# High and low parts of queries and keys side by side in one staging tile, sent to both rows of a pair by one transfer

## The chip, the cores and the metric

The kernel runs on one core of a Trainium2 chip. The metric is the device time of one execution in microseconds (us). The profile names the engines PE (TensorE; PEld is its weight load), DVE (VectorE), ACT (ScalarE), POOL (GpSimd) and SP (SyncE, which here only issues transfers); "SPq" is SyncE's issue queue.

## What is computed

Two layers of a transformer block over x (4 sequences of 512 tokens, width 320) with a context (4 sequences of 1601 tokens, width 192); 20 heads of width 16. Each layer is self-attention, cross-attention and a gated feed-forward, each behind a layer norm and added to x:

```python
h1 = _ln(x, n1_g, n1_b)
x = _attn(h1, h1, q1, k1, v1, o1_w, o1_b, heads) + x
h2 = _ln(x, n2_g, n2_b)
x = _attn(h2, context, q2, k2, v2, o2_w, o2_b, heads) + x
h3 = _ln(x, n3_g, n3_b)
a, g = jnp.split(h3 @ ff_w1 + ff_b1, 2, axis=-1)
return a * jax.nn.gelu(g, approximate=False) @ ff_w2 + ff_b2 + x
```

where `_attn` is `softmax(q @ k.T * 16**-0.5) @ v` per head, then the output projection. All in float32.

## The kernel before, in words

**Units.** The work is a list of units: one for each layer, kind (self or cross), sequence and group of four heads, so 40 self units and 40 cross units, and 8 feed-forward units. `main` runs a unit as a loop over chunks of 128 keys: 4 in a self unit, 13 in a cross unit. Each chunk is two rounds, and a feed-forward unit has 24, which makes 2 x (20 x 8 + 20 x 26 + 4 x 24) = 1552 rounds in the program. A round is also the clock of the schedule: `clock["round"]` counts them, and due times and gaps are given in rounds.

**High and low parts.** Scores need float32 accuracy, but the matmuls of scores run in the single-pass type float32r. So queries and keys are split in two parts, high = the rounded value and low = the rest, and the sum of four products (high and low of the one by high and low of the other) is accumulated. A head has 16 dimensions and owns 32 partitions: each dimension owns a pair of rows. In the key tile `kT` the even row of a pair holds the high part and the odd row the low part. The query tile `q` has two slots `e`: in slot 0 even rows hold high and odd rows low, in slot 1 the other way round. A matmul over 32 rows with slot 0 gives high x high + low x low, and one with slot 1 adds the two mixed products.

**From projection to rows.** Projections come out of PSUM with one row for each dimension, not a pair. ScalarE (`L919` in self units, `L952` in cross units) or, for the keys of a cross unit, VectorE or ScalarE (`L1011`, `L1014`) writes the value into a staging tile, and `split` on GpSimd makes high (`L820`) and low (`L821`) of it. High and low are two tiles of their own, `high` and `low`, two buffers each (`two`), for self units and for the queries of cross units; for the keys of cross units they are two parts, `room["high"]` and `room["low"]`, of one larger tile that the trace calls `stages`. The staging tile of a unit has 64 rows for each thing that is moved: rows 0 to 63 are queries and 64 to 127 keys in a self unit; in a cross unit the two halves of rows are the two halves of the tokens. Transfers then spread the 64 rows over the 128 rows of pairs. Each transfer takes either high or low to every second row:

- self unit: keys 2 transfers (`kT<-high`, `kT<-low`, 128 KB each), queries 4 (two slots, high and low, 128 KB each);
- cross unit: keys 4 (two halves of 801 keys, high and low, 200.2 KB each), queries 8 (two halves of the tokens, two slots, high and low, 64 KB each).

All these are issued at one line, `L869`, in `move`.

**The schedule around it.** `move` doesn't issue at once: it puts a function on one of two lists of the unit (`u.moves["k"]`, `u.moves["q"]`). `carry`, called once a round, issues from these lists in order when the buffer is free (`may`) and a gap has passed (`GAP` = 3 rounds after the split for the first move of a list). It has a room of 4 and each move takes 2, so at most two moves go out in a round; what room is left goes to errands, such as the loads of finished heads and the `nrows` transfers. During start-up (`start["on"]`) moves go out at once, in turn on the queues of SyncE and ScalarE. `u.open` counts a unit's moves that are still to go: 3 in a self unit and 6 in a cross unit, since one move holds two transfers. When it is 0, `u.when` is set to the round, and four rounds later (`at_hand`) `giver` may hand out the unit's first products, the row maxima (`sps` by `L1073` and `L1098`, reduced by VectorE in `L1084`), which run beside the scores (`st` by `L1321`) of the unit before. `staging_free` lets the next projection but one start when a unit's query moves have gone out. The negated row maxima get to the score products as a third matmul with `nrows`, which comes by four small transfers at `L1168` for each unit.

**Order.** The program order on each engine is fixed when the kernel is built, from `pace`, `pick` and the costs written in the code; the chip only waits on semaphores. SyncE's queue takes its transfers strictly in program order: moves, `nrows` (`L1168`), `oway` (`L1188`, finished heads to DRAM), `aT` and `rT` (`L1221`, `L1222`, back from there), context tiles (`L725`, `L758`, `L772`) and weights.

Of the kernel before, what the change touches and what calls it, by code (L numbers as in the profile page):

```python
# [9 lines left out]
F32 = mybir.dt.float32  # L10
# [7 lines left out]
B, N, D = 4, 512, 320  # L18
S2, CTX = 1601, 192
H, DH = 20, 16  # L20
# [3 lines left out]
P = 128  # L24
NQ = N // P
G, HG = 5, 4
GD = HG * DH
SLOT = 32
# [14 lines left out]
HALF = TOK // 2  # L43
# [6 lines left out]
GAP = 3  # L50
# [28 lines left out]
def kernel(ctx: ExitStack, tc: tile.TileContext, x, context, ws, out):  # L79
# [18 lines left out]
    nc = tc.nc  # L98
# [42 lines left out]
    def take_rooms(l):  # L141

        room["layer"] = l

        for i in range(1, 3):
            kbuf[i] = shared.tile([P, KW], F32R, tag=f"kT{i}", name=f"kT{i}")
        qbuf[3] = shared.tile([P, 2, N], F32R, tag="rests", name="q3")
        free = shared.tile([P, NHC * D], F32, tag="second", name="stages")
        at = 0

        def part(n):
            nonlocal at
            at += n
            return free[:, at - n : at]

        room["low"], room["high"] = part(HALF), part(HALF)
        room["in"] = [part(2 * CTX).rearrange("p (c d) -> p c d", d=CTX) for _ in range(2)]
        room["turned"] = [part(2 * CTX).rearrange("p (k w) -> p k w", k=KB) for _ in range(2)]
        room["context"] = [
            w1_flat[:96, 2 * D : 2 * D + 2 * TOK].rearrange("p (k w) -> p k w", k=2),  # L160
            one.tile([96, 2, TOK], F32, tag="ctxT", name="ctxT"),
        ]
# [138 lines left out]
    class Unit:  # L301


        def __init__(self, l, kind, b, g):
            self.l, self.kind, self.b, self.g = l, kind, b, g
            self.cross = kind == "cross"
            self.rows_of = None
            self.nkeys = S2 if self.cross else N
            self.nch = (self.nkeys + P - 1) // P

            self.moves = {"k": deque(), "q": deque()}
            self.moving = {"k": 0, "q": 0}
            self.open = 6 if self.cross else 3
            self.keyed = None
            self.when = None
            self.vmade = [0, 0]

            self.made = {"q": 0, "k": 0, "kv": 0}
            self.scored = 0
            self.valued = 0  # L320
            self.steps = 2 * self.nch if kind != "ff" else 2 * NHC + NQ
            self.before = None
            self.others = []
            self.early = False
            self.own = {}
            self.pairs = self.hT = self.kvT = None
# [5 lines left out]
        @property  # L332
        def q(self):
            if not self.cross and self.m % 4 == 3:
                return kbuf[2][:, N : 3 * N].rearrange("p (e n) -> p e n", e=2)
            return qbuf[3 if self.early else self.m % 3 if self.cross else self.m % 4]

        def places(self):

# [483 lines left out]
    def add_proj(u):  # L823
# [28 lines left out]
            else:  # L852
                add(chain, 0.0, hold, due - 4, yes, lambda: "h" in u.own)

        def staged():
            users.append(u)
            return (two.tile([P, N], F32, tag=n, name=n) for n in ("low", "high"))

        def move(of, pairs, may, gap=0):

# [22 lines left out]
        def keys_free():  # L883
            return not pending["k"]

        def move_queries(high, low, cols, may, gap):
            for e in range(2):
                move(
                    "q", lambda e=e: [(u.q[(e + h) % 2 :: 2, e, cols], t) for h, t in enumerate((high, low))],
                    may, 0 if e else gap,  # L890
                )

        def both(part):

            w = N // 2
            at = part * w
            ps = bank("qkps")
            written(1.4, ps)
            busy("act", 0.4, ps)
            for k, _, n in HK:  # L900
                for f, m in tiles_of(P):
                    column = u.g * GD + f % GD
                    nc.tensor.matmul(  # L903
                        ps[f : f + m, :w],
                        lhsT=wqk[:n, k, f // GD, column : column + m],
                        rhs=first.hT[:n, k, at : at + w],
                        start=(k == 0),
                        stop=(k == 2),
                    )
            if part == 0:  # L910
                u.stage = tuple(staged())
            low, high = u.stage
            if u.i == 0:
                nc.scalar.activation(high[:, at : at + w].bitcast(F32R), ps[:, :w], AF.Copy, scale=scales[:, 0:1])
                nc.vector.scalar_tensor_tensor(
                    low[:, at : at + w], ps[:, :w], scales[:, 0:1], high[:, at : at + w], ALU.mult, ALU.subtract
                )
            else:
                nc.scalar.activation(low[:, at : at + w], ps[:, :w], AF.Copy, scale=scales[:, 0:1])  # L919
            if part == 0:  # L920
                return
            if u.i:
                split(low, high)
            def may():
                return unread() and free()

            move(
                "q", lambda: [(u.kT[h::2, u.k0 : u.k0 + N], t[GD:]) for h, t in enumerate((high, low))], may, GAP,
            )
            move_queries(high[:GD], low[:GD], slice(0, N), may, 0)  # L930
            u.keyed = True
            first.made["q"] += 1
            first.made["k"] += 1

        def queries():

            w = N // 2
            ps = bank("qps")
            written(1.41, ps)
            busy("act", 0.33, ps)  # L940
            for k, _, n in HK:
                for i in range(2):
                    for f in range(GT):
                        nc.tensor.matmul(  # L944
                            ps[(i * GT + f) * SLOT : (i * GT + f + 1) * SLOT, :w],
                            lhsT=wq2[:n, k, u.g * GD + f * SLOT : u.g * GD + (f + 1) * SLOT],
                            rhs=first.hT[:n, k, i * w : (i + 1) * w],
                            start=(k == 0),
                            stop=(k == 2),
                        )  # L950
            low, high = staged()
            nc.scalar.mul(low[:, :w], ps[:, :w], DH**-0.5)  # L952
            split(low[:, :w], high[:, :w])
            for i in range(2):
                rows = slice(i * GD, (i + 1) * GD)
                move_queries(high[rows, :w], low[rows, :w], slice(i * w, (i + 1) * w), unread, 0 if i else GAP)
            u.keyed = True
            first.made["q"] += 1

        def keys_of_context(part):  # L960

            at, w = KCUT[part]
            ps = bank("kps")
            written(0.1 + w * 4 * 2 / 2400, ps)
            for k in range(2):
                for i in range(2):
                    for f in range(GT):
                        nc.tensor.matmul(  # L968
                            ps[(i * GT + f) * SLOT : (i * GT + f + 1) * SLOT, :w],
                            lhsT=wk2[:, k, u.g * GD + f * SLOT : u.g * GD + (f + 1) * SLOT],  # L970
                            rhs=first.kvT[:, k, i * HALF + at : i * HALF + at + w],
                            start=(k == 0),
                            stop=(k == 1),
                        )
            low, high = room["low"], room["high"]
            taken(low[:, at : at + w], ps[:, :w], ps, 0.12 + w * 0.001)
            if part + 1 < len(KCUT):
                return
            split(low, high)

            def half(i):
                to = u.kT[:, i * HALF : (i + 1) * HALF]
                return [(to[h::2], t[i * GD : (i + 1) * GD]) for h, t in enumerate((high, low))]

            move("k", lambda: half(0), free, GAP + 1)
            move("k", lambda: half(1), free)
            first.made["kv"] += 1
# [69 lines left out]
    def max_pairs(u):  # L1057
# [9 lines left out]
        def one_tile(j, t, s):  # L1067
# [4 lines left out]
            def product(e):  # L1072
                nc.tensor.matmul(  # L1073
                    own[0][:, :w],
                    lhsT=u.q[j * SLOT : (j + 1) * SLOT, e, t * P : (t + 1) * P],
                    rhs=u.kT[j * SLOT : (j + 1) * SLOT, u.k0 + at : u.k0 + at + w],
                    start=(e == 0),
                    stop=(e == 1),
# [10 lines left out]
        def rest_tiles(heads):  # L1089
# [5 lines left out]
            def product(t):  # L1095
                for e in range(2):
                    for j, ps in zip(heads, pss):
                        nc.tensor.matmul(  # L1098
                            ps[:, t * w : (t + 1) * w],
                            lhsT=u.q[j * SLOT : (j + 1) * SLOT, e, t * P : (t + 1) * P],  # L1100
                            rhs=u.kT[j * SLOT : (j + 1) * SLOT, at : at + w],
                            start=(e == 0),
                            stop=(e == 1),
# [204 lines left out]
    def main(u, give, nxt):  # L1308
# [6 lines left out]
        def score(c, j):  # L1315
# [4 lines left out]
            def product(e):  # L1320
                nc.tensor.matmul(  # L1321
                    own[0][:r, :],
                    lhsT=ones[rows, :r] if e == 2 else u.keys(rows, c),
                    rhs=u.rows[rows, :] if e == 2 else u.q[rows, e, :],
                    start=(e == 0),
                    stop=(e == 2),
                )
# [442 lines left out]
```

## Time and profile before

| | us |
|---|---|
| median of 3 runs | 2936.93 |
| lowest and highest | 2933.56, 2943.3 |
| profiled execution, its own time | 2939.09 |
| its span in the profile | 2937.3 |
| TensorE busy (98% of the span) | 2875.8 |
| VectorE busy (70%) | 2062.3 |
| ScalarE busy (64%) | 1884.9 |
| GpSimd busy (44%) | 1289.8 |
| DMA queue of SyncE: share of 16 engines' span | 24.6% |
| bytes that it moved | 182.11 MB |

How to read it: the span is the time from the first to the last instruction; the profiled execution's own time lies 1.8 us above it, and 2.2 us above the median of the runs. A busy TensorE is not TensorE at its peak: its matmuls are pipelined, and its granted clock (mean 0.993 in this execution) can be half of full speed in places.

### The profile page before, as it was taken

To read this page: it belongs to the slowest core of one execution; us is meant where nothing else is said; L and a number is where in the kernel's file an instruction comes from. 1 tells how busy PE (TensorE), PEld (TensorE's weight loads), DVE (VectorE), ACT (ScalarE), POOL (GpSimd) and SP (SyncE) were. 2 spreads that over 40 slices of the span, in tenths; PEclk is the share of its full clock that TensorE was granted. 3 is DMA by queue.
4 is the path that set the end of the run, shared out by engine and by line. 5 is a ranking of instruction groups with operands and counts; after the bars stand their busy time and mean duration, and the time that the engine had idled before them with its cause. 6 is when DMAs were issued, how large, how long until landed. Compare 5 with 4: busy or idle time off the path is not lost.

```text
span 2937.3 us, 84400 instructions
## 1 busy us (share of the span) xinstructions
PE 2875.8 (98%) x35018; PEld 1540.1 (52%) x35018; DVE 2062.3 (70%) x4048; ACT 1884.9 (64%) x3737; POOL 1289.8 (44%) x1409
## 2 busy tenths in 40 slices
PE   8999999999999999999999999999999999999999
PEld 4545555555555555355554555555555555544554
DVE  7767888888888878323258778888888888873221
ACT  3767677887887878601138776778888788783000
POOL 3556345555555545211215663455455564451110
PEclk8999999999999999999999999999999999999999
DMA  4444224232232212200113342222221121222000
GB/s 107 107 121 101 68 69 106 57 83 63 50 94 63 51 53 62 79 22 11 42 36 90 102 102 69 64 63 54 54 65 47 50 72 47 58 54 77 20 22 14
DMA packets 186543, 188.70 MB, mean 64 GB/s; under 512 B 69668, under 2 KB 137264, under 8 KB 186160
## 3 DMA queue, kind: packets, MB, share of 16 engines
q1 hardware_dynamic: 185368, 182.11, 24.6%
q8 instruction: 276, 4.52, 0.6%
q10 hardware_dynamic: 760, 1.18, 0.2%
q14 instruction: 107, 0.88, 0.1%
q0 software_dynamic: 32, 0.00, 0.0%
HBM read 55.76 MB, written 29.36 MB: 29 GB/s over the span
## 4 chain that ended last, share of the span: by engine, by line
PE 86%; DVE 6%; POOL 2%; issue 2%; ACT 2%; DMA 1%; SPq 1%; POOLq 0%; ACTq 0%; DVEq 0%
PE av L1347 22%; PE st L1321 19%; PE fps L1432 10%; PE sps L1073 9%; PE yps L1539 6%; PE vps L1032 5%; PE kps L968 3%; PE ops L1247 3%; DVE nmax L1084 3%; PE qkps L903 3%; PE fps L1492 3%; DVE pm L1084 2%; PE qps L944 2%; PE sps L1098 1%; ACT pr L1331 1%
## 5 line engine op out<-in xcount | busy, mean ns | idle before, releaser
L1331 ACT ACTIVATE pr<-st 128x512 f32<-128x512 f32 (+1 forms) x2720 | 1405.3, 603 | 393.7 <-PE st L1321 358.6
L1084 DVE TENSOR_REDUCE pm<-sps 128x1 f32<-128x512 f32 (+1 forms) x1920 | 1146.8, 660 | 147.0 <-PE sps L1073 137.4
L1367 POOL TENSOR_TENSOR o<-o,vo 128x512 f32<-128x512 f32 x576 | 740.2, 1285 | 952.3 <-ACT vo L1366 930.4
L1073 PE MATMUL sps<-kT,q 32*128 32x512 f32 (+1 forms) x4800 | 871.6, 422 | 13.3 <-DMA q<-low 3.2
L1321 PE MATMUL st<-q,kT 32*128 32x512 f32 (+1 forms) x5120 | 785.9, 421 | 3.1 <-ACT low L919 2.6
L1347 PE MATMUL av<-pr,vals 128*32 128x512 f32 (+1 forms) x5440 | 737.8, 608 | 25.4 <-ACT pr L1331 9.3
L1321 PEld LDWEIGHTS st<-q,kT 32*128 32x128 f32 (+1 forms) x5120 | 441.6, 180 | 293.5 <-issue 112.1
L1321 PE MATMUL st<-nrows,ones 32*128 32x512 f32 (+1 forms) x2720 | 557.6, 400 | 8.6 <-DMA nrows<-turned 8.5
L1073 PEld LDWEIGHTS sps<-kT,q 32*128 32x128 f32 x4800 | 431.0, 184 | 81.6 <-ACT pr L1331 12.7
L1084 DVE TENSOR_REDUCE nmax<-sps 128x1 f32<-128x512 f32 x640 | 396.2, 681 | 101.8 <-PE sps L1073 95.5
L1366 ACT COPY vo<-av 128x512 f32<-128x512 f32 x576 | 351.8, 611 | 27.6 <-PE av L1347 21.8
L1503 ACT ACTIVATE gl<-fps,b 128x512 f32<-128x512 f32 x80 | 54.8, 687 | 414.2 <-PE fps L1492 303.0
L1432 PE MATMUL fps<-hT,w 128*128 128x512 f32 x640 | 283.0, 597 | 0.0
L1321 PEld LDWEIGHTS st<-nrows,ones 32*128 32x128 f32 (+1 forms) x2720 | 261.2, 180 | 21.7 <-issue 9.5
L1347 PEld LDWEIGHTS av<-pr,vals 128*32 128x32 f32 (+1 forms) x5440 | 111.3, 108 | 300.2 <-DVE pm L1084 161.6
L1504 DVE SCALAR_TENSOR_TENSOR hid<-fps,b,gl 128x512 f32<-128x512 f32 x80 | 59.7, 748 | 240.9 <-ACT gl L1503 238.8
L1432 PEld LDWEIGHTS fps<-hT,w 128*128 128x128 f32 x640 | 119.3, 190 | 155.3 <-issue 153.3
L1539 PE MATMUL yps<-w,hid 128*128 128x320 f32 x640 | 176.3, 435 | 0.1
L1539 PEld LDWEIGHTS yps<-w,hid 128*128 128x128 f32 x640 | 120.4, 190 | 56.5 <-ACT gl L1503 5.3
L1247 PEld LDWEIGHTS ops<-wo,aT 112*32 112x32 f32 (+1 forms) x3072 | 98.1, 110 | 59.8 <-issue 31.8
L1247 PE MATMUL ops<-wo,aT 112*32 112x160 f32 (+1 forms) x3072 | 125.0, 301 | 1.4 <-POOL aT L1229 1.1
L520 POOL TENSOR_SCALAR root<-root 128x4 f32<-128x4 f32 x22 | 5.2, 237 | 263.8 <-DVE root L514 263.3
(91 smaller groups left out, 2531.2 us busy)
## 6 DMA issues: line engine op xcount, KB each, us to landing
kT<-stages SPq DMA_DIRECT2D x160, 200.2 KB
oway<-o SPq DMA_DIRECT2D x80, 256.0 KB
q<-high SPq DMA_DIRECT2D x160, 64.0 KB
q<-low SPq DMA_DIRECT2D x160, 64.0 KB
kT<-high SPq DMA_DIRECT2D x60, 128.0 KB
q<-high SPq DMA_DIRECT2D x60, 128.0 KB
kT<-low SPq DMA_DIRECT2D x57, 128.0 KB
aT<-oway SPq DMA_DIRECT2D x32, 224.0 KB
```

Source lines behind the costliest of these rows:

```text
L903: nc.tensor.matmul(ps[f : f + m, :w], lhsT=wqk[:n, k, f // GD, column : column + m], rhs=first.hT[:n, k, at : at + w], start=(k == 0), sto ...
L1032: nc.tensor.matmul(ps[f : f + m, :w], lhsT=u.kvT[:n, k, at + f : at + f + m], rhs=wv[:n, k, h0 * DH : h1 * DH], start=(k == 0), stop=(k == ...
L1073: nc.tensor.matmul(own[0][:, :w], lhsT=u.q[j * SLOT : (j + 1) * SLOT, e, t * P : (t + 1) * P], rhs=u.kT[j * SLOT : (j + 1) * SLOT, u.k0 + ...
L1084: nc.vector.tensor_reduce(to, own[0][:, :w], AX.X, ALU.max)
L1247: nc.tensor.matmul(ps[f : f + m, : D // 2], lhsT=aT[:n, k, f * NQ + t * SLOT : f * NQ + t * SLOT + m], rhs=wo[:n, k, cols], start=(k == 0) ...
L1321: nc.tensor.matmul(own[0][:r, :], lhsT=ones[rows, :r] if e == 2 else u.keys(rows, c), rhs=u.rows[rows, :] if e == 2 else u.q[rows, e, :], ...
L1331: nc.scalar.activation(p[:r], own[0][:r], AF.Exp)
L1347: nc.tensor.matmul(ps[j * SLOT : (j + 1) * SLOT, :], lhsT=columns_of[:r, head : head + SLOT], rhs=pr.pop((c, j))[:r, :], start=True, stop= ...
L1366: nc.scalar.copy(vo, ps)
L1367: nc.gpsimd.tensor_tensor(u.o, u.o, vo, ALU.add)
L1432: nc.tensor.matmul(ps, lhsT=w1[:, k, i * FF + c * P : i * FF + (c + 1) * P], rhs=natural(u.hT[:, k]), start=start, stop=stop,)
L1539: nc.tensor.matmul(ps[:, :D], lhsT=hid[c][:, t * P : (t + 1) * P], rhs=w2[:, c, :], start=(c == 0), stop=(c == NHC - 1),)
```

## The change

High and low get one staging tile, `halves`, with high and low side by side in each row (`[128, 2, n]`). For the keys one transfer takes the 64 rows with both parts to the 128 rows of `kT`: high of row p to row 2p, low to row 2p + 1. For the queries one transfer takes the two parts of row p, one behind the other, to row 2p and again to row 2p + 1 (the source is read twice by a broadcast). So both rows of a pair now hold high in slot 0 and low in slot 1, and the two matmuls give (high + low of the key) x high and x low of the query: the same four products. In a cross unit the two halves of the tokens lie one behind the other, each with its high and low, so a slot is no longer one run of 512 columns but two runs of 256; `queries` makes that view. It is read by `st` (`L1321`, as the moving operand, whole slot) and by `sps` (`L1073`, `L1098`, as weights, 128 columns at a time, one run as before). A self unit now has 2 transfers (keys 256 KB, queries 512 KB) and a cross unit 4 (keys 400.5 KB each, queries 256 KB each). A move holds one transfer, so `open` starts at 2 and 4. The room in `carry` is as before.

```diff
-        room["low"], room["high"] = part(HALF), part(HALF)
+        room["halves"] = part(2 * HALF).rearrange("p (d n) -> p d n", d=2)
...
-            self.open = 6 if self.cross else 3
+            self.open = 4 if self.cross else 2
...
+        def queries(self, rows, e, t=None):
+            if not self.cross:
+                return self.q[rows, e, :] if t is None else self.q[rows, e, t * P : (t + 1) * P]
+            q = self.q.rearrange("p d n -> p (d n)").rearrange("p (i d n) -> p d i n", i=2, d=2)
+            return q[rows, e] if t is None else q[rows, e, t // 2, t % 2 * P : (t % 2 + 1) * P]
...
-        def staged():
+        def staged(w):
             users.append(u)
-            return (two.tile([P, N], F32, tag=n, name=n) for n in ("low", "high"))
+            return two.tile([P, 2 * N], F32, tag="halves", name="halves")[:, : 2 * w].rearrange("p (d n) -> p d n", d=2)
...
-        def move_queries(high, low, cols, may, gap):
-            for e in range(2):
-                move(
-                    "q", lambda e=e: [(u.q[(e + h) % 2 :: 2, e, cols], t) for h, t in enumerate((high, low))],
-                    may, 0 if e else gap,
-                )
+        def move_queries(halves, cols, may, gap):
+            n = halves.shape[0]
+            src = halves.rearrange("p (o d) n -> p o (d n)", o=1).to_broadcast([n, 2, 2 * halves.shape[2]])
+            move("q", lambda: [(u.q.rearrange("p d n -> p (d n)")[:, cols], src)], may, gap)
...
-            move(
-                "q", lambda: [(u.kT[h::2, u.k0 : u.k0 + N], t[GD:]) for h, t in enumerate((high, low))], may, GAP,
-            )
-            move_queries(high[:GD], low[:GD], slice(0, N), may, 0)
+            move("q", lambda: [(u.kT[:, u.k0 : u.k0 + N], u.stage[GD:])], may, GAP)
+            move_queries(u.stage[:GD], slice(0, 2 * N), may, 0)
...
-                move_queries(high[rows, :w], low[rows, :w], slice(i * w, (i + 1) * w), unread, 0 if i else GAP)
+                move_queries(halves[rows], slice(i * N, (i + 1) * N), unread, 0 if i else GAP)
...
             def half(i):
-                to = u.kT[:, i * HALF : (i + 1) * HALF]
-                return [(to[h::2], t[i * GD : (i + 1) * GD]) for h, t in enumerate((high, low))]
+                return [(u.kT[:, i * HALF : (i + 1) * HALF], room["halves"][i * GD : (i + 1) * GD])]
...
-                    rhs=u.rows[rows, :] if e == 2 else u.q[rows, e, :],
+                    rhs=u.rows[rows, :] if e == 2 else u.queries(rows, e),
```

More of the change, by code (lines that the diff above doesn't have):

```diff
@@ L910, in both @@
             if part == 0:
-                u.stage = tuple(staged())
-            low, high = u.stage
+                u.stage = staged(N)
+            high, low = (u.stage[:, d] for d in range(2))
             if u.i == 0:
@@ L950, in queries @@
                         )
-            low, high = staged()
-            nc.scalar.mul(low[:, :w], ps[:, :w], DH**-0.5)
-            split(low[:, :w], high[:, :w])
+            halves = staged(w)
+            high, low = (halves[:, d] for d in range(2))
+            nc.scalar.mul(low, ps[:, :w], DH**-0.5)
+            split(low, high)
             for i in range(2):
                 rows = slice(i * GD, (i + 1) * GD)
-                move_queries(high[rows, :w], low[rows, :w], slice(i * w, (i + 1) * w), unread, 0 if i else GAP)
+                move_queries(halves[rows], slice(i * N, (i + 1) * N), unread, 0 if i else GAP)
             u.keyed = True
@@ L974, in keys_of_context @@
                         )
-            low, high = room["low"], room["high"]
+            high, low = (room["halves"][:, d] for d in range(2))
             taken(low[:, at : at + w], ps[:, :w], ps, 0.12 + w * 0.001)
@@ L1074, in product @@
                     own[0][:, :w],
-                    lhsT=u.q[j * SLOT : (j + 1) * SLOT, e, t * P : (t + 1) * P],
+                    lhsT=u.queries(slice(j * SLOT, (j + 1) * SLOT), e, t),
                     rhs=u.kT[j * SLOT : (j + 1) * SLOT, u.k0 + at : u.k0 + at + w],
@@ L1099, in product @@
                             ps[:, t * w : (t + 1) * w],
-                            lhsT=u.q[j * SLOT : (j + 1) * SLOT, e, t * P : (t + 1) * P],
+                            lhsT=u.queries(slice(j * SLOT, (j + 1) * SLOT), e, t),
                             rhs=u.kT[j * SLOT : (j + 1) * SLOT, at : at + w],
```

## The prediction

> **What bounds the kernel now.** I read the page first, then TensorE's waits, then the chain of waits in the stretches where TensorE stood still, and last the issue queue of SyncE in those stretches.
>
> ```profile
> PE 2875.8 (98%) x35018; PEld 1540.1 (52%) x35018; DVE 2062.3 (70%) x4048; ACT 1884.9 (64%) x3737; POOL 1289.8 (44%) x1409
> PE 86%; DVE 6%; POOL 2%; issue 2%; ACT 2%; DMA 1%; SPq 1%; POOLq 0%; ACTq 0%; DVEq 0%
> ```
>
> TensorE is busy for 2875.8 of 2937.3 us and carries 86% of the chain. The change takes no matmul away, so all it can win is in the 61.5 us in which TensorE is idle (2937.3 - 2875.8), or in time in which it is busy but slow. DMA and SyncE's queue carry 1% of the chain each. Who ends TensorE's idle time:
>
> ```profile
> PE av L1347 <- ACT pr L1331: 9.3, 40, 0.3
> PE st L1321 <- DMA nrows<-turned: 8.5, 8, 3.0
> PE sps L1073 <- DMA q<-low: 3.2, 1, 3.2
> PE st L1321 <- ACT low L919: 2.6, 1, 2.6
> ACT low L919 <- DMA q<-low: 11.9, 3, 5.3
> ```
>
> The columns are microseconds in all, times, and the longest. Three rows touch the change. The 3.2 us is one wait of the very first unit for its queries. The 2.6 us is one wait in which ScalarE, with work for TensorE queued behind it, was itself held (last row, longest 5.3) until the transfer of an older unit's low part had left the staging tile. The 8.5 us are waits for the small `nrows` transfers, which stand in SyncE's queue behind whatever was issued before them. After the two long waits TensorE also runs slowly for a while:
>
> ```profile
> 171.86:175.26 3.40, 3.22 (x20) 1.30 (x24) 1.47 (x3) 2.07 (x4) 2.91 (x9) 0.50 0.74 176
> 202.58:209.40 6.82, 6.82 (x67) 3.59 (x65) 1.61 (x3) 3.30 (x7) 3.13 (x3) 0.50 0.12 38
> 1062.74:1069.55 6.81, 6.81 (x52) 3.05 (x54) 4.08 (x7) 4.21 (x9) 2.51 (x2) 0.50 0.07 9
> 198.50:201.00 2.50, 1.04 (x13) 0.49 (x11) 1.29 (x2) 0.00 (x0) 0.00 (x0) 1.00 0.89 204
> 1061.72 0.50 PE L1321 MATMUL st<-nrows,ones 32*128 32x512 f32 x2 [1.60 <-DMA nrows<-turned]
> ```
>
> The first four rows are stretches with the busy time of TensorE, its weight loads, VectorE, ScalarE and GpSimd; the third number from the right is the granted clock: 0.50 for 3.40 us after the wait that ended at 172, and for 6.82 us after the one that ended at 202. Half clock loses half of the stretch: 1.7 and 3.4 us, 5.1 us together. The third stretch, behind the wait of 1.60 us in the last row, shows that so short a wait cost as much.
>
> **What the change takes away.** Each unit's `move` calls become fewer: a self unit issues 2 transfers where it issued 6, a cross unit 4 where it issued 12. With 40 units of each kind that is 240 instead of 720 issues, over the same bytes. One issue holds SyncE's queue for about 0.6 us:
>
> ```profile
> L869 SPq DMA_DIRECT2D q<-high x220: 461/594/2311, 18.4 to 2583.3; - x110
> L869 SPq DMA_DIRECT2D kT<-stages x160: 471/542/2983, 236.0 to 2565.8; - x160
> ```
>
> 480 fewer at 0.54 to 0.59 us is some 270 us of SyncE's queue. Nearly all of that lies beside other work: a unit's queries and keys go out long before they are read. What it is worth is decided at the two places where the chain goes through this queue. The first:
>
> ```profile
> 154.18 0.53 SPq L869 DMA_DIRECT2D kT<-high  x1
> ...
> 157.31 2.31 SPq L869 DMA_DIRECT2D q<-high  x1
> 159.67 0.60 SPq L869 DMA_DIRECT2D q<-low  x1
> 160.36 0.59 SPq L1188 DMA_DIRECT2D oway<-o  x1
> ...
> 163.94 4.32 SPq L1168 DMA_DIRECT2D nrows<-turned  x4
> 172.04 0.79 PE L1321 MATMUL st<-nrows,ones 32*128 32x512 f32 x2 [3.04 <-DMA nrows<-turned]
> ```
>
> Between 154.18 and 160.36 stand six moves of one unit; after the change two. Saved: one key issue and three query issues. [...] The second place:
>
> ```profile
> 194.76 0.54 SPq L869 DMA_DIRECT2D kT<-high  x1
> 195.99 1.78 SPq L869 DMA_DIRECT2D q<-high  x1
> 199.09 2.39 DMA q<-low
> 201.65 0.84 ACT L919 ACTIVATE low<-qkps,scales 128x256 f32<-128x256 f32 x2 [5.27 <-DMA q<-low]
> 202.17 0.50 PE L1321 MATMUL st<-q,kT 32*128 32x512 f32 x2 [2.63 <-ACT low L919]
> 190.00:202.00 12.00, 9.42 (x171) 5.74 (x159) 6.34 (x14) 4.41 (x9) 4.82 (x6) 1.00 0.67 172
> ```
>
> The third row is of the chain: the last of six issues began at 199.09 and landed 2.39 us later, which freed ScalarE. Afterwards the only query transfer is issued right behind the keys, near 195.4, but it carries 512 KB. While only query transfers moved (198.50 to 201.00, above) the engines ran 0.89 full at 204 GB/s, so 512 KB need 2.6 us where the last 128 KB need 0.65: 1.9 us longer to land. If the issue isn't held: 195.4 + 2.39 + 1.9 = 199.7, 1.8 us sooner than 201.5. If it is held as now (1.2 us over the usual 0.59): 200.9, 0.6 sooner. Middle 1.2; the wait of 2.63 us shrinks to 1.4.
>
> The Trainium skill (SBUF — State Buffer, "The DMA setup-cost knee") gives 138 GB/s for transfers of 64 KiB and 224 for 256 KiB, so by it a cross unit's 512 KB of queries would take 2.3 instead of 3.8 us, an estimate from that page. The 204 GB/s above, with transfers of 128 KB one behind the other, speak against so much.
>
> Clock: the waits that are left (1.1 and 1.4 us) lie just under the 1.60 us that dropped the clock at 1062. I count half of the 5.1 us: 2.6. The page that bears on it is the Trainium skill's TensorE: Matmul & The Clock Gate, "The HAM clock gate": the clock falls after at least one idle window of about 3.4 us. By that rule waits of 1.1 and 1.4 us would cost no clock, all 5.1 us would come back, and the sum below would be 2.5 us larger; but here 3.04, 2.63 and 1.6 us sufficed, so the trace is harsher than the rule.
>
> **What the change adds or moves, at no cost.** The transfer now waits for the low part too, one GpSimd subtraction later:
>
> ```profile
> L821 POOL TENSOR_TENSOR low<-low,high x79: 725/740/1298, 22.8 to 2578.6; 128x256 f32<-128x256 f32 x40, 128x512 f32<-128x512 f32 x39
> L821 POOL TENSOR_TENSOR stages<-stages x40: 1597/1603/1624, 223.9 to 2558.4; 128x801 f32<-128x801 f32 x40
> 20.00:40.00 20.00, 14.54 (x156) 6.87 (x160) 18.32 (x52) 2.32 (x6) 4.64 (x6) 0.66 0.44 109
> ```
>
> At most 1.30 us for a self unit or a cross unit's queries, 1.6 us for a cross unit's keys. The low-part issue that followed it in the same queue waited for the same thing, so nothing behind it leaves later. Cover: three rounds of gap, about 1.9 us each (2937.3 us over 1552 rounds). At the start there is no gap: unit 0 waits for both parts anyway, and ScalarE, which issues every other transfer there, is free sooner; VectorE is busy 18.32 of the 20 us that follow (last row, third engine) and sets the pace, so I count 0, with one subtraction, 1.3 us, to either side as ends.
>
> Fewer moves empty a unit's list one round sooner, so its first products may be handed out a round (1.9 us) sooner. In the long middle they are handed out in time already; 0.
>
> In cross units the moving operand of `st` becomes two runs of 256 columns, in 40 x 13 x 2 = 1040 slots of four row groups. What a broken run costs:
>
> ```profile
> L1432 PE MATMUL fps<-hT,w 128*128 128x512 f32 x640 | 283.0, 597 | 0.0
> L1539 PE MATMUL yps<-w,hid 128*128 128x320 f32 x640 | 176.3, 435 | 0.1
> ```
>
> `fps` reads sixteen runs of 32 columns, `yps` one run of 320: 283.0/640/512 = 0.864 ns and 176.3/640/320 = 0.861 ns per column. Sixteen runs cost 1.5 ns per matmul at most, two about nothing: 0. Neither is of the single-pass type (float32r) that `st` has, and no row shows that with a broken run.
>
> **Sum.** 1.9 + 1.2 + 2.6 = 5.7 us less, say 6; with the ends of the terms 2.5 (1.9 + 0.6, no clock back) to 10.8 (3.04 + 2.63 + 5.1). The profiled execution took 2939.09 us, its span 2937.3; the median shown is 2936.93. So 2933 for that execution, 2931 for the median.
>
> **Rivals.** What a measurement of this kernel can tell from no change is about 0.3%, 8.8 us: faster means under 2928.1, slower over 2945.7.
>
> [...]
>
> 2. *Queries are read before they land* (slower). A unit counts as at hand four rounds after its last issue. That issue now comes a round sooner, and the bytes behind it are four times as many (1.9 us more). Where SyncE is held up by GpSimd's split, TensorE reaches the queries first. Place: units whose split is late. It decides from the point where SyncE lags by more than about 4 us (7.6 us of rounds, less 2.6 for the bytes and the 1.1 of the landing that are neither issue nor bytes, 2.39 - 0.59 - 0.65).
>
> ```profile
> SPq L869 <- POOL high L820: 171.0, 31, 28.3
> ```
>
> That is 5.5 us on average, so such lags exist; against it, only the very first unit shows a wait for queries now. A wait of 2.6 us with its clock drop costs 6.0; three make 18: 2931 + 18 = 2949.
>
> 3. *A broken run costs TensorE.* From 8.5 ns per slot (8.8 us / 1040) it would decide. The upper end, a run that costs as much as the 0.07 us that a slot has beside its columns (0.23 us, less 512 columns at 0.315 ns, by the medians below), is 73 us, 3004.
>
> ```profile
> L1098 PE MATMUL sps<-kT,q x1280: 215/271/325, 368.4 to 2626.4; 32*128 32x128 f32 x183
> L1073 PE MATMUL sps<-kT,q x4800: 354/392/792, 23.0 to 2623.1; 32*128 32x512 f32 x138, 32*128 32x450 f32 x54
> 881.32 0.39 PE L1321 MATMUL st<-q,kT 32*128 32x512 f32 x2
> 881.55 0.44 PE L1321 MATMUL st<-nrows,ones 32*128 32x512 f32 x2
> ```
>
> (392 - 271) ns over 384 columns is 0.315; two products of one row group start 0.23 us apart.
>
> 4. *The change does not bring the data sooner.* If the bytes alone set the landing, both waits stay: 2937.
>
> **Chances.** Forecast 0.38, rival 1 0.37, rival 2 0.15, rival 3 0.07, rival 4 0.03. So faster by over 0.3%: 0.37; within: 0.38 + 0.03 = 0.41; slower: 0.22. The likeliest case gives 2931, by its ends 2926 to 2935. The range takes in rival 1 to its end and rival 2: 2917 to 2950; rival 3's upper part is left out.
>
> **What would show it.** Right: 240 issues on the move line; the waits near 172 and 202 at 0 to 1.5 us, the half-clock stretches behind them gone or shorter; `st` and `sps` groups with the same means as now. Rival 2 would show as new waits of `sps` or `st` for the DMA of the queries away from the start, each with half clock behind it. Rival 3 would show as a longer spacing of `st` in cross units and the same in self units. The forecast is wrong if TensorE's idle time falls by less than 2 us or grows, or if its busy time moves by more than the 5 us that the clock explains.

## The result: 0.2% slower, and the profile after

The changed kernel takes 2944.3 us (median of 22 runs, 2939.7 to 2949.7); the kernel before, run beside it, takes 2937.16 us (22 runs, 2932.97 to 2943.3). The ratio is 1.0021 [1.0014, 1.0027], so 4 to 8 us slower. That lies within 0.3% and within the forecast's range, but on the other side of the forecast's 6 us gain. The profiled execution of the changed kernel took 2940.83 us and is a low one among its runs; it lies only 1.7 us over the profiled execution of before. The search for the cause below therefore goes by places in the trace, and the sizes go by the ratios of many runs.

The page after, in the lines that answer to those of before: busy time of each engine, and the shares of the chain that ended last.

```profile
PE 2866.7 (98%) x35018; PEld 1538.1 (52%) x35018; DVE 2066.0 (70%) x4052; ACT 1881.4 (64%) x3733; POOL 1299.7 (44%) x1409
PE 86%; DVE 5%; DMA 3%; ACT 2%; issue 2%; POOL 1%; SPq 0%; ACTq 0%; POOLq 0%; DVEq 0%
```

TensorE does the same 35018 matmuls and is idle for 72.3 us (2939.0 - 2866.7) instead of 61.5: idle time grew by 10.8 us, while its busy time fell by 9.1. DMA has 3% of the chain instead of 1%. Who ends TensorE's idle time, and what ScalarE waited for before it wrote to a staging tile (microseconds in all, times, longest):

```profile
PE sps L1076 <- ACT halves L924: 13.3, 7, 7.3
PE st L1324 <- DMA nrows<-turned: 6.4, 7, 1.5
PE sps L1076 <- DMA q<-halves: 4.5, 1, 4.5
ACT halves L924 <- DMA q<-halves: 19.2, 5, 9.6
ACT halves L924 <- DMA kT<-halves: 7.0, 3, 3.5
```

The wait of 3.0 us for `nrows` is gone, but the wait for ScalarE's write to the staging tile in self units, which was 3.7 us in three pieces (2.6 and 1.1 for two), is now 13.3 us in seven pieces, the longest 7.3. ScalarE itself waits 26.2 us there for transfers to leave the tile, where it was 15.3 (11.9 for queries, 3.4 for keys). The two largest places, from the timeline (start, duration, instruction, wait before it):

```profile
174.05 1.48 PE L908 MATMUL qkps<-hT,wqk 128*32 128x256 f32 x24
178.60 0.47 ACT L924 ACTIVATE halves<-qkps,scales 128x256 f32<-128x256 f32 x1 [3.54 <-DMA kT<-halves]
179.12 0.49 PE L1076 MATMUL sps<-kT,q 32*128 32x512 f32 x1 [2.47 <-ACT halves L924]
191.30 5.70 SPq L779 DMA_DIRECT2D w<-ctxT  x8
193.34 1.48 PE L908 MATMUL qkps<-hT,wqk 128*32 128x256 f32 x24
197.72 0.61 SPq L876 DMA_DIRECT2D q<-halves  x1
203.54 0.47 ACT L924 ACTIVATE halves<-qkps,scales 128x256 f32<-128x256 f32 x1 [9.61 <-DMA q<-halves]
204.06 0.79 PE L1076 MATMUL sps<-kT 32*128 32x512 f32 x2 [7.30 <-ACT halves L924]
```

`qkps` is the projection of queries and keys. Its result goes to a staging tile; there are two, so before ScalarE writes one, the transfers of the unit before last must have emptied it. At 193.34 TensorE makes a projection whose tile is still full: its query transfer leaves SyncE only at 197.72, behind eight transfers at `L779`, and lands 5.7 us later. ScalarE stands at the write for 9.61 us with the other work for TensorE queued behind it, and TensorE stands for 7.30 us. In the kernel before, the projections of these two units stand elsewhere in TensorE's program order:

```profile
178.47 1.48 PE L903 MATMUL qkps<-hT,wqk 128*32 128x256 f32 x24
180.02 0.47 ACT L919 ACTIVATE low<-qkps,scales 128x256 f32<-128x256 f32 x1 [0.42 <-PE qkps L903]
195.27 2.78 PE L903 MATMUL qkps<-hT,wqk 128*32 128x256 f32 x48
```

There the projection at 178.47 found its tile empty (ScalarE waited 0.42 us, for the projection itself), and the one at 195.27 comes behind a chunk's `av` that in the changed kernel comes after it. In the changed kernel these projections stand one chunk sooner in TensorE's program, and in program order the first half of a projection comes sooner in 22 of the 40 self units (by one chunk in 20, by two in 2). So the time seems to go into an order, not into a transfer. Two theories say why:

- **Gate.** `staging_free` opens when the query list of the unit before last is empty. A self unit's list had three moves (one of keys, two of queries) and now has two, a cross unit's four and now two; two moves go out at a time. So the gate opens a chunk sooner, the projection is placed a chunk sooner, and its data meets a tile whose transfer has only just been issued.
- **Landing.** The order is innocent; a transfer of 512 KB holds the tile until its last byte, where four of 128 KB freed it sooner.

A third effect was open: the first products of a unit may be handed out sooner (`u.when`), since `open` starts at 2 and 4.

### The profile page after: what moved, and what is told of

Read it like the earlier page. It is cut to its first block, busy times and chain, and to the rows that moved or that the text cites. A ratio compares the mean times of both kernels' runs of the same rounds, so it can differ in the third digit from the quotient of the medians.

```text
span 2939.0 us, 83447 instructions
## 1 busy us (share of the span) xinstructions
PE 2866.7 (98%) x35018; PEld 1538.1 (52%) x35018; DVE 2066.0 (70%) x4052; ACT 1881.4 (64%) x3733; POOL 1299.7 (44%) x1409
## 4 chain that ended last, share of the span: by engine, by line
PE 86%; DVE 5%; DMA 3%; ACT 2%; issue 2%; POOL 1%; SPq 0%; ACTq 0%; POOLq 0%; DVEq 0%
PE av L1350 22%; PE st L1324 19%; PE fps L1435 10%; PE sps L1076 9%; PE yps L1542 6%; PE vps L1035 5%; PE kps L972 3%; PE ops L1250 3%; PE qkps L908 3%; PE fps L1495 3%; DVE nmax L1087 2%; ACT pr L1334 2%; PE qps L947 2%; DMA q<-halves 2%; DVE pm L1087 1%
## 5 line engine op out<-in xcount | busy, mean ns | idle before, releaser
L1076 PE MATMUL sps<-kT,q 32*128 32x450 f32 (+1 forms) x4800 | 869.3, 422 | 14.8 <-ACT halves L924 6.0
L1369 ACT COPY vo<-av 128x512 f32<-128x512 f32 x576 | 353.4, 614 | 13.6 <-PE av L1350 10.9
L1549 DVE TENSOR_TENSOR x<-yps,x 128x320 f32<-128x320 f32 x32 | 15.7, 491 | 149.9 <-PE yps L1542 149.9
## 6 DMA issues: line engine op xcount, KB each, us to landing
kT<-stages SPq DMA_DIRECT2D x80, 400.5 KB
```

The costliest lines, as they stand in the source:

```text
L1076: nc.tensor.matmul(own[0][:, :w], lhsT=u.queries(slice(j * SLOT, (j + 1) * SLOT), e, t), rhs=u.kT[j * SLOT : (j + 1) * SLOT, u.k0 + at : u ...
L1369: nc.scalar.copy(vo, ps)
```

## The experiments

All ratios are to the kernel before, run in the same rounds on the same chip, with a 95% interval. Diffs are to the changed kernel unless said otherwise.

### The old order with the new transfers

```diff
-            self.open = 4 if self.cross else 2
+            self.open = 6 if self.cross else 3
...
             move("q", lambda: [(u.q.rearrange("p d n -> p (d n)")[:, cols], src)], may, gap)
+            move("q", lambda: [], may, 0)
```

An empty move behind every query move makes the lists as long as before. TensorE's program is then, instruction for instruction, that of the kernel before.

> The merged transfers stay; empty moves fill the lists up to the old number (3 in a self unit, 6 in a cross unit), so every due time, gap and gate falls in the rounds in which it fell before the change. Theory G (the lists empty a round sooner, so the next projection but one is placed a round sooner and ScalarE is sent into a wait for a staging tile whose transfer has just left): the wait near 200 us shrinks from 7.3 to about 3 us, ratio to the kernel before 1.000 to 1.001. Theory L (the large transfer itself lands late, 5 to 6 us after its issue where the last small one took 2.4): the wait stays, ratio 1.002.

Measured: 2936.73 us, 0.9995 [0.9987, 1.0004]. The loss is gone with the order; what is left is no gain that can be told from nothing. Its waits, from the timeline:

```profile
170.04 0.50 PE L1325 MATMUL st<-nrows,ones 32*128 32x512 f32 x2 [1.32 <-DMA nrows<-turned]
194.25 1.61 SPq L876 DMA_DIRECT2D q<-halves  x1
200.51 0.84 ACT L925 ACTIVATE halves<-qkps,scales 128x256 f32<-128x256 f32 x2 [5.68 <-DMA q<-halves]
201.04 0.73 PE L1325 MATMUL st<-q,kT 32*128 32x512 f32 x3 [3.07 <-ACT halves L925]
```

Here the two places of the prediction can be read as it meant them. The first wait fell from 3.04 to 1.32. At the second, ScalarE got its tile at 200.51 instead of 201.65, 1.1 us sooner; yet TensorE's wait didn't shrink (3.07 after 2.63), because TensorE had come 1.6 us sooner itself.

### The new order with the old transfers

```diff
-            move("q", lambda: [(u.q.rearrange("p d n -> p (d n)")[:, cols], src)], may, gap)
+            def pairs():
+                flat = u.q.rearrange("p d n -> p (d n)")[:, cols]
+                return [(flat[o::2, d * w : (d + 1) * w], halves[:, d]) for o in range(2) for d in range(2)]
+            move("q", pairs, may, gap)
```

The keys likewise: one move, but 720 issues in all.

> The changed kernel with its new lists and rounds, but each transfer is issued in the old pieces (high and low apart, each row of a pair apart; 720 issues). Theory G: ratio stays at 1.0015 to 1.002, with only the start-up repaired (1.6 us). Theory L: ratio 1.000, the wait near 200 us back at 2.6 us.

Measured: 2946.73 us, 1.0032 [1.0021, 1.0043]. TensorE's waits:

```profile
PE sps L1089 <- ACT halves L932: 15.8, 8, 8.1
PE st L1337 <- DMA nrows<-turned: 9.2, 9, 3.1
```

With small transfers in the new order the wait for the staging tile is there as well, and a little longer (8.1 us). The loss is larger than either theory expected, but its interval overlaps that of the changed kernel. So the landing theory falls: the loss comes with the order, whatever the size of the transfers.

### Old pieces in start-up alone, in the new and in the old order

```diff
+                if start["on"]:
+                    return [(flat[o::2, d * w : (d + 1) * w], halves[:, d]) for o in range(2) for d in range(2)]
+                return [(flat, src)]
```

> The changed kernel; only the three units of the start-up send their keys and queries in the old pieces, in turn on the queues of SyncE and ScalarE. Both theories: the first wait for queries goes from 4.5 back to 3.2 us and the kernel gains the 1.6 us by which it is late at 52 us: ratio 1.0015 to 1.002. If the start-up makes no difference to the end, 1.002.

> Old clock (empty moves) and old pieces in the start-up, merged transfers everywhere else. Theory G: 0.999 to 1.000, nothing left of the loss. Theory L: 1.0015.

Measured: new order 2941.8 us, 1.0015 [1.0006, 1.0025], which overlaps the changed kernel's interval; old order 2933.45 us, 0.9981 [0.9972, 0.999], against 0.9995 without the pieces. One pair shows nothing that can be told, the other 4 us (0.0014 of 2937), with intervals that just overlap. I come back to this below.

### The gate alone, held

```diff
+        def sent():
+            return len(users) < 2 or users[-2].when == -9 or clock["round"] >= users[-2].moving["q"] + 4
...
-            add(chain, (0.477,) * 3, queries, due - 2, staging_free)
+            add(chain, (0.477,) * 3, queries, due - 2, staging_free, sent)
```

The same for self units. Only the projection is held, until four rounds after the last query move of the unit before last (start-up excepted); the lists, the room of `carry` and the time at which products are handed out stay as in the changed kernel.

> The changed kernel as it is (no empty moves, room and at-hand time new); only the projection of the next unit but one is held until four rounds (two chunks) after the last query transfer of the unit whose staging tile it takes, as it fell before the change in self units. Theory G: like the old clock, ratio 0.999 to 1.0005. If the room in carry or the earlier at-hand time does the harm, it stays at 1.002.

Measured: 2933.59 us, 0.9988 [0.998, 0.9997]. Holding one condition turns 1.0021 into 0.9988, 10 us; in 38 of the 40 self units the projection then stands at the chunk where it stood before the change. So neither the sooner handing out nor the room costs time by itself; the gate does.
What is left of the second wait:

```profile
203.65 0.73 PE L1327 MATMUL st<-q,kT 32*128 32x512 f32 x3 [2.95 <-ACT halves L927]
```

2.95 us, about the 2.63 of the kernel before; 7.30 without the hold.

### The gate alone, opened

The old list lengths and the old handing out (the empty moves of the first experiment), but `staging_free` looks only at real moves:

```diff
-            return len(users) < 2 or not users[-2].moves["q"]
+            return len(users) < 2 or all(m[3] for m in users[-2].moves["q"])
```

(`m[3]` marks an empty move.)

> Merged transfers with empty moves that take room and count for the at-hand time as before; only the staging tile counts as free as soon as the real moves have gone. Theory G: all of the loss, ratio 1.0015 to 1.0025, the wait near 200 us at 6 us or more. Its rival (room and at-hand time): 1.000.

Measured: 2957.41 us, 1.0068 [1.0055, 1.008]. The direction is the gate's, the size is not what was expected: three times the changed kernel's loss.

```profile
206.47 0.47 ACT L925 ACTIVATE halves<-qkps,scales 128x256 f32<-128x256 f32 x1 [11.36 <-DMA q<-halves]
207.00 0.79 PE L1077 MATMUL sps<-kT 32*128 32x512 f32 x2 [9.03 <-ACT halves L925]
1651.21 0.49 PE L1077 MATMUL sps<-kT,q 32*128 32x512 f32 x1 [1.75 <-ACT halves L925]
1754.72 1.16 PE L1077 MATMUL sps<-kT,q 32*128 32x512 f32 x2 [3.20 <-ACT halves L925]
```

The wait is at the same place, 9.03 instead of 7.30 us, and there are more of the kind, above all at 1651 and 1754, with 3.4 and 6.8 us of half clock there. In the traces the excess lies at these places: the chunk whose `av` starts at 285.9 in the kernel before starts 12.9 us later here and 6.3 later in the changed kernel, and between the chunks at 1537.5 and 1854.2 this kernel loses another 10.9 us and the changed one 1.8. Why this order, so near to the changed kernel's, brings these further waits and loses some 14 us more stays open. Opening the gate sooner is enough for the loss, but the loss depends on the order that comes of it.

### The gate held further, with and without merged transfers

> The held projection, and old pieces in the start-up. Theory G: 0.998 to 0.999, like the old clock with old pieces in the start-up.

> The same with the projection held six rounds. If the wait near 200 us (2.9 us that are left under the old clock) comes from the same cause, it goes as well: 0.997. If later projections come too late for the products that need them, it gives that back: 0.999 or more.

> The order of TensorE's work is that of the kernel with the projection held six rounds and start-up in pieces (0.9975, line for line the same order), but every transfer goes in the old pieces, 720 issues. If the order alone makes the gain, this kernel takes the same time, 0.997 to 0.998. If the merged transfers have a worth of their own (2.6 us by the pair of old order and old order with merged transfers, in the profiles rather 6.5), it is 2.6 to 6.5 us slower than that: 0.9985 to 0.9997, with a longer nrows wait.

> Projection held six rounds, all transfers merged, start-up too. Against the same with start-up in pieces (0.9975): if the start-up term is real, +1.1 us (four rounds, with and without pieces) to +3.3 us (old order, with and without): 0.9979 to 0.9986; if it is only chance, 0.9975. The 3 us wait near 200 us that four rounds left should be gone here, as it was with pieces.

> Projection held eight rounds, one more step than six. If waits of ScalarE for its staging tile are all that is to win, six rounds have won it and eight give the same, 0.997 to 0.998. If the later projection begins to delay the products that read its queries, TensorE waits for queries away from the start, and it is slower: over 0.9985.

| projection held | start-up | later transfers | median us | ratio |
|---|---|---|---|---|
| 4 rounds | pieces | merged | 2932.47 | 0.9985 [0.9976, 0.9994] |
| 6 rounds | pieces | merged | 2929.45 | 0.9975 [0.9965, 0.9985] |
| 6 rounds | pieces | pieces | 2929.48 | 0.9967 [0.9954, 0.9979] |
| 6 rounds | merged | merged | 2931.41 | 0.9973 [0.9964, 0.9983] |
| 8 rounds | pieces | merged | 2930.23 | 0.9972 [0.9961, 0.9984] |

The edits are the gate's, with 4, 6 or 8 for the number of rounds, put on the changed kernel or on those with pieces. The three kernels with six rounds have the same program on TensorE, instruction for instruction. From four rounds to six this wait goes too. Of the kernel with all transfers merged, the timeline of the place and the granted clock (third number from the right) over the same 48 us, first of this kernel, then of before:

```profile
180.94 2.78 PE L911 MATMUL qkps<-hT,wqk 128*32 128x256 f32 x48
182.49 0.47 ACT L927 ACTIVATE halves<-qkps,scales 128x256 f32<-128x256 f32 x1 [0.54 <-PE qkps L911]
172.29 0.50 PE L1327 MATMUL st<-nrows,ones 32*128 32x512 f32 x2 [0.22 <-DMA nrows<-turned]
160.00:208.00 48.00, 44.77 (x672) 25.01 (x668) 35.49 (x80) 33.49 (x66) 35.27 (x47) 1.00 0.58 149
```

```profile
160.00:208.00 48.00, 41.14 (x572) 21.74 (x568) 30.53 (x67) 27.34 (x55) 29.14 (x41) 0.91 0.50 130
```

ScalarE waits for the projection alone, TensorE's two waits are 0.22 us and nothing, and the clock stays full where it was 0.91; TensorE starts 672 matmuls in the stretch instead of 572. Eight rounds give nothing more and take nothing away, as the first of the two views of that run said.

The third row of the table speaks against a worth of the merged transfers: in one and the same order, 720 issues give 0.9967 and 240 give 0.9973. Expected was that the pieces lose 2.6 to 6.5 us; they don't. All six-round kernels beat both the kernel before and the changed one, by 7 to 10 us against before; which of them is best these runs can't tell.

## Why the prediction was wrong

**The step that failed** is the sentence on the emptying of the lists: "Fewer moves empty a unit's list one round sooner, so its first products may be handed out a round (1.9 us) sooner. In the long middle they are handed out in time already; 0." It saw the right event and followed it to one reader only, `u.when`. The list has a second reader, `staging_free`, which places the projection of the next unit but one. That reader was named in the description of the kernel, and its cost was left at nothing, without a reason. The size was wrong as well: `carry` is called when a chunk's round of fill work ends, once for every two rounds, and not once a round as the description ahead of the prediction says, so what goes sooner goes by a chunk, two rounds. The runs show that this term is a loss of 8 to 10 us: 7.6 against the old order with the new transfers (1.0021 to 0.9995), 9.7 against the gate held alone (1.0021 to 0.9988). It makes up some 8 of the 12 us by which the forecast missed (5.7 us less expected, 6.2 more by the ratio); the other 4 are the forecast's own terms, which follow.

**The forecast's own terms**, by the run that has the new transfers in the old order:

- The first wait: forecast 1.1 us left, measured 1.32. Right in size, though no run shows the term of 1.9 us as a count of issues, nor why one issue took 2.31 us: here `nrows` leaves 1.3 us sooner (162.68 for 163.94), with issues of 1.27 and 1.92 us between the moves and it, and the wait ends 2.0 us sooner (170.04 for 172.04). The issue of 2.31 us, from 157.31 to 159.62 in the kernel before, ended with the DMA engines all but idle (a share of 0.05 over the 0.65 us that follow). In the changed kernel the wait is 0.6 us.
- The second: the landing was forecast between 199.7 and 200.9, and ScalarE wrote at 200.51. Right, but partly by luck: the queries left at 194.25 where about 195.4 was assumed, and took 6.2 us to land where the working had 4.3 (5.5 with the issue held). And the 1.2 us were added to the first term, but they don't add. TensorE comes to the second place sooner by what it won at the first, and so waits longer there for the same landing: 2.63 - 1.1 + 1.6 = 3.1, measured 3.07. What the first wait gives is kept only as far as the second doesn't take it back.
- The clock: forecast 2.6 us back. Half clock in the old order with new transfers:

```profile
171.30:174.70 3.40, 3.40 (x36) 1.76 (x39) 1.64 (x4) 2.16 (x5) 2.98 (x8) 0.50 0.97 232
202.00:205.40 3.40, 3.33 (x21) 1.29 (x25) 1.29 (x2) 2.17 (x6) 1.30 (x2) 0.51 0.14 46
```

6.8 us instead of 10.2, so 1.7 us back. Half clock still came behind the wait of 1.32 us, as the prediction feared from the 1.60 us at 1062. The Trainium skill (TensorE: Matmul & The Clock Gate, "The HAM clock gate") has the clock fall after an idle window of about 3.4 us; the trace does not agree. But the length of one wait doesn't decide it either. With the projection held six rounds and start-up in pieces, a longer wait left the clock full:

```profile
1792.68 0.50 PE L1339 MATMUL st<-nrows,ones 32*128 32x512 f32 x2 [1.86 <-DMA nrows<-turned]
1788.00:1800.00 12.00, 10.12 (x143) 5.25 (x146) 8.70 (x17) 7.80 (x16) 5.03 (x4) 1.00 0.18 60
```

So what a wait of 1 to 2 us costs in clock couldn't be had from the one row at 1062.

- The sum of these was forecast as 5.7 us. The chunk whose `av` starts at 271.2 in the kernel before (its row is shown below) starts at 269.0 here, so 2.2 us are won by then, and the many runs give 1.5 us with an interval that holds zero:

```profile
L1351 PE MATMUL av<-pr,vals x8: 592/604/617, 269.0 to 269.5; 128*32 128x512 f32 x8
```

- In the order with six rounds the same merge is worth nothing (0.9973 against 0.9967), and in the changed kernel's it is worth 3 us by the medians, not clear of noise (1.0021 against 1.0032). So I count the direct gain of fewer issues as 0 to 4 us, not 6; the old order's interval ends at 3.8.

**The broken run of 256 columns** was forecast at 0, and is 0. The products keep their median of 392 ns (first before, then after), and the stretch from 271 to 983, nearly all cross units, has the same length in the kernel before and in the changed one (further down):

```profile
L1321 PE MATMUL st<-q,kT x5120: 382/392/791, 45.0 to 2660.2; 32*128 32x512 f32 x197
```

```profile
L1324 PE MATMUL st<-q,kT x5120: 382/392/792, 46.6 to 2661.9; 32*128 32x512 f32 x197
```

```profile
L1347 PE MATMUL av<-pr,vals x8: 592/604/617, 271.2 to 271.7; 128*32 128x512 f32 x8
L1347 PE MATMUL av<-pr,vals x8: 592/605/617, 983.2 to 983.6; 128*32 128x512 f32 x8
```

```profile
L1350 PE MATMUL av<-pr,vals x8: 592/605/617, 278.3 to 278.8; 128*32 128x512 f32 x8
L1350 PE MATMUL av<-pr,vals x8: 592/605/617, 989.8 to 990.3; 128*32 128x512 f32 x8
```

(First before, then after, the same two chunks in each.) 712.0 us before and 711.5 after. The stretch holds 182 chunks of cross units, 364 of the 1040 slots; the 8.5 ns per slot from which the third rival would decide would make 3.1 us in it.

**How large the loss is at its place.** The same rows give 278.3 - 271.2 = 7.1 us, and it doesn't grow further (6.6 at the second pair). 1.7 of it are there at the chunk that starts at 159.1 before and at 160.8 after, and 5.4 come between. Busy time of the engines over this stretch, first before, then after:

```profile
159.10:271.20 112.10, 103.09 (x1528) 57.21 (x1520) 76.23 (x159) 72.39 (x146) 68.90 (x93) 0.95 0.44 111
```

```profile
160.80:278.30 117.50, 103.70 (x1576) 57.77 (x1568) 76.86 (x158) 73.55 (x150) 71.25 (x95) 0.96 0.41 106
```

TensorE's idle time grew from 9.0 to 13.8 us, by 4.8 of the 5.4. The waits above make most of it: 2.47 and 7.30 for ScalarE and 0.6 for `nrows`, where 2.63 and 3.04 stood. The clock is no part of it in these two executions (0.95 and 0.96). Over many runs it may be: the changed kernel's mean granted clock is 0.9925 in its 22 runs, that of the kernel before 0.9933 to 0.9937 in the rounds of the experiments, and 0.0008 to 0.0012 of 2937 us is 2 to 4 us. Behind this stretch the two run alike up to 1062, where the kernel before waits 1.60 us and drops its clock for 6.8 us, and the changed one waits 0.91 us and doesn't. The chunk that starts at 1125.7 before starts at 1127.2 after, so 5 of the 7 us come back there. The other drops in the later part:

```profile
1523.46:1530.28 6.82, 6.82 (x45) 2.70 (x46) 5.87 (x13) 3.83 (x8) 2.03 (x2) 0.51 0.06 11
```

```profile
2303.60:2310.43 6.83, 6.83 (x56) 2.93 (x52) 3.53 (x7) 4.05 (x9) 2.50 (x2) 0.50 0.05 4
```

Before has two such drops, the one at 1062 that the prediction shows and the one at 1523 (first row), after has one (second row). In the execution with the old order and the new transfers, which runs the same program on TensorE as before, only the one near 1516 is left, so these late drops aren't fixed to an order. What came back at 1062 is why this pair of executions shows 1.7 us; that the many runs show 4 to 8 because such drops fall differently in them is likely and not shown.

**Start-up** was forecast at 0 with 1.3 to either side. The first wait for queries went from 3.2 to 4.5 us, and TensorE's clock over the start was lower, first before, then after:

```profile
18.50:52.00 33.50, 26.79 (x363) 13.81 (x352) 28.35 (x70) 7.53 (x19) 8.14 (x10) 0.80 0.33 84
```

```profile
18.50:52.00 33.50, 28.64 (x352) 15.39 (x348) 27.36 (x68) 6.49 (x16) 6.30 (x8) 0.69 0.32 81
```

But the merged kernel with six rounds shows a clock of 0.90 in the same stretch, and pieces in start-up, tried in four orders, gained 0.0006, 0.0014, 0.0003 and -0.0002 of the time. Only the second comes near to what the intervals can tell. So the start-up's cost isn't settled: small, 2 us or less in three of four.

**The rivals.** The second was on the right side, with a late tile and half clock behind it, but in the wrong direction of the transfer: it had TensorE reading queries that had not landed, and what happened was ScalarE writing where queries had not left. No run shows a wait for queries away from start-up that is new. The first rival, that both waits vanish and the clock stays full, gave 2926; the six-round order comes near it (2929 to 2931), by another cause than fewer issues. The signs that the text named did their work: 240 issues at the move line (107 + 80 + 50 + 3), the means of `st` and `sps` unchanged, and idle time that grew by 10.8 us where a fall of 2 was the limit. That busy time fell by 9.1 at the same time was not foreseen; two late clock drops against one explain 3.4 of it, and the rest stays open.

## What to carry to other kernels

When a change makes a list, a counter or a queue shorter, find every condition in the build-time schedule that reads its length, and ask for each what it lets start sooner; a start that is allowed sooner on an in-order engine is a risk, not a gift, since everything behind it waits if its buffer isn't free. To judge the change itself, run it once with the order of before pinned (here: empty entries in the lists) and once the other way round; here that pair told order from transfer. And don't add the gains of two waits that follow each other in one chain: what is won at the first is partly waited for at the second.

## What the runs showed of the hardware that was not expected

One transfer of 512 KB from 64 partitions landed 5.7 to 6.2 us after its issue began (5.71 at 197.72 in the changed kernel; from 194.25 to 200.41 in the old order, of which 1.6 us were the issue). The end of the chain in the trace, of the changed kernel:

```profile
197.72 5.71 DMA q<-halves
203.43 0.02 issue
203.54 0.48 ACT halves L924
```

Four transfers freed the tile no sooner in the end, since the tile is free only when the last has landed, and 480 issues fewer on SyncE, some 270 us of its queue, were worth 1.5, 3 and -2 us in the three orders that were tried, none clear of noise. Half clock of 3.4 us followed a wait of 1.32 us in one execution and stayed away behind one of 1.86 us in another.
